# Attention and a mixture of experts on one core: the experts moved inside the branch, the second half ordered by hand, projections a slot later

## The chip, the cores and the metric

The kernel runs on one core of a Trainium2 chip (trn2). A core has a matrix engine (TensorE, PE), a vector engine (VectorE, DVE), a scalar engine with function tables (ScalarE, ACT), GpSimd (POOL), a queue engine that only issues transfers (SyncE, SP), an on-chip memory of 128 partitions (SBUF) and an accumulator memory of 8 banks (PSUM). The engines run on their own and wait for each other through semaphores. All data are float32. The metric is the time of one execution on the device, in microseconds (us).

## The reference

`x` is one sequence of 2048 rows of 512. The reference is an attention layer with residual and layer norm, and then a mixture of experts with residual and layer norm:

```python
q, k = unit_norm(q), unit_norm(k)           # 16 heads of 32; rotary positions on every second head
logits = einsum("bshd,bthd->bhst", q, k) * q_gain
y = causal_softmax(logits) @ v
x = layernorm(x + y @ w_out)
scores = softmax(x @ gate_w)                # 8 experts, the best 2 of each row
routed = sum over the 2 of  w_e * (silu(x @ w_gate[e]) * (x @ w_up[e])) @ w_down[e]      # 352 hidden
shared = (silu(x @ sw_gate) * (x @ sw_up)) @ sw_down                                     # 704 hidden
x = layernorm(x + routed + shared)
```

## The kernel before

**Attention.** `attention_then_moe` (L1384 on) loads `x` and the weights, works out whether the gains are small enough for a softmax with a fixed shift, and branches on it (`tc.If`, L1517). With the inputs here the first arm runs, `fast_attention`; the other, `general_attention`, is code that is jumped over. `sparse_moe` stands behind both arms.

`fast_attention` works in slots. Slot `n` is one unit of 160: a head group `g` of 4 heads, a block `b` of 512 queries, a tile `kt` of 128 keys. In a slot, PE makes the scores (L331), ACT the exponentials (L341), POOL the causal mask on the diagonal (L352), DVE and POOL the running sums (L370), and PE the product with the values (L379). Every engine runs in the order in which the code is written (`manual_schedule`, L477). Beside this, odd slots take one long step from `queue` (`long_step`, L443: a projection into q, k and v for a tile, L126, or, in the last head group, an output projection, L229), and even slots one short step from `shorts` (transposes, L204 and L271, and gates). `later(k, what)` puts a piece of work `k` slots on. A block's last value product starts `normalize` (L391): the sums over partitions (L397), their reciprocal, and `divide` (L417, L419). In the last head group `divide` puts the block's four output projections into `queue` at once (L426). In this phase, projections and transposes share one PSUM bank. When the last q, k, v projection is out of the queue, `x_is_read` (L450) loads the shared expert's weights into the place of the transposed `x`. After slot 160 a tail does what is left, filled up with six pieces of the shared expert's first block (`fillers`).

**Experts.** `sparse_moe` first finds each row's two experts and sorts the rows by expert (DVE, from L802). Meanwhile the shared expert's first half runs: eight tiles of 128 rows in blocks of two (`BT`); `shared_up(b, j)` makes piece `j` of 6 of the hidden rows (L667 on PE, L678 or L686 on ACT, L680 on DVE), and `shared_down(b)` the output (L975, and L981 for the last chunk, of half height). Then 36 tiles of routed rows are gathered, multiplied and written to `yd` in memory (`routed`, L1119). A second, inner branch (L1162) is for more tiles than usual, and isn't taken here.

The second half of the shared expert (L1169 on) takes blocks 4 to 7, and with them the rows of the first half whose shared part is kept in `accd`. For each of 16 tiles, `with_experts` (L1046) gathers the two expert rows with POOL's indirect transfers (L1049) and adds them on DVE (L1052); `finish` (L1054) normalizes on DVE (`layer_norm`, L779: two statistics, and a root by eleven small steps, L602 to L607) and stores (L1056). In slot 0 of each block SP reads the block's rows, the old rows and the next block's transposed rows (`read_block`, L948, 512 KB). Here only PE and SP run in the written order (`in_order`, L1079); for the other engines a planner chooses it. `yd` rows have 4 buffers (`m4`), the rows of `x` and of the sums 5 (`m5`).

Of the kernel before, what the change touches and what calls it, by code (L numbers as in the profile page):

```python
# [16 lines left out]
P = 128  # L17
S = 2048
DM = 512
# [22 lines left out]
def fast_attention(  # L42
    tc, mem, xT, xa, x, x1d, wq_sb, wo_sb, gain, rope_sb, gw, logits, ident, neg_gmax, small, x_is_read,
    x1T_kept, x1T_done, more_pieces,
):
# [13 lines left out]
    with (  # L59
# [331 lines left out]
        def normalize(g, b, y):  # L391
# [25 lines left out]
            def divide(rec, sign):  # L417
                by_tile = lambda a: a.rearrange("p (t m) -> p t m", t=TPB)
                nc.vector.scalar_tensor_tensor(  # L419
                    xa[:, b * TPB : (b + 1) * TPB, g * P : (g + 1) * P], by_tile(y), sign, by_tile(rec), ALU.mult, ALU.mult  # L420
                )
                if g == NC - 1:
                    if b == 0:
                        fetch(0)
                        fetch(1)
                    queue.extend((None, project(b * TPB + tl)) for tl in range(TPB))  # L426

# [15 lines left out]
        def long_step(n):  # L443
            if not queue or not may_start(queue[0][0], n):
                return False
            for step in queue.pop(0)[1]:
                step()
            if not read and (not queue or queue[0][0] is None):
                read.append(n)
                x_is_read()  # L450
            return True
# [25 lines left out]
        with tc.manual_schedule():  # L477
# [14 lines left out]
            banks(0, 2, 3)  # L492
            x_transposed(0)[0]()
            for i in range(EARLY * TPB):
                now[0] = i - EARLY * TPB
                tile_step(i)
                for what in due.pop(now[0], []):
                    what()
                for _ in range(2):
                    short_step(now[0])  # L500
# [6 lines left out]
            while n < NU or pending or queue or shorts or ends or due:  # L507
# [57 lines left out]
                n += 1  # L565
            assert not fillers

# [123 lines left out]

HID0 = 5 * GW

# [17 lines left out]
def sparse_moe(tc, big, shared, xs, ident, logits, w_gate, w_up, w_down, x1d, x1Td, x1T_kept, yd, accd, out):  # L711
# [12 lines left out]
    with (  # L724
# [10 lines left out]

        ones = mc.tile([P, P], F32, name="mones")
        nc.gpsimd.memset(ones, 1.0)

# [6 lines left out]

        hid_lent = [hidden(lent(CH * W)) for _ in range(2)]
        lent_early = lent(2 * P)
        last_down = big[:, DOWNS + (NE - 1) * DW :]
# [8 lines left out]
        nc.gpsimd.iota(table[:, 0, :], [[P, NTILES]], base=0, channel_multiplier=0)  # L757
        tile_starts = mc.tile([P, NTILES], F32, name="tile_starts")
        nc.vector.tensor_copy(tile_starts, table[:, 0, :])
# [18 lines left out]

        def layer_norm(dst, src, name):  # L779
            stats = m2.tile([P, 6], F32, tag="ln_stats", name=f"stats{name}")  # L780
            nc.vector.bn_stats(stats, src)  # L781
            mv = m2.tile([P, 2], F32, tag="ln_mv", name=f"mv{name}")
            nc.vector.bn_aggr(mv, stats)
            rstd = m2.tile([P, 1], F32, tag="ln_rstd", name=f"rstd{name}")
            inv_sqrt(nc, m2, rstd, mv[:, 1:2], EPS_LN, f"ln{name}")
            nc.vector.tensor_scalar(dst, src, mv[:, 0:1], rstd, ALU.subtract, ALU.mult)  # L786


# [14 lines left out]
        nc.scalar.activation(sc, sc, AF.Exp)  # L803
        rsum = mc.tile([P, NT], F32, name="rsum")
        nc.vector.reciprocal(rsum, reduced(sc, ALU.add, "lsum"))
# [146 lines left out]
        def hid_of(b):  # L952
            if b == 0:
                return hidden(big[:, HID0 : HID0 + CH * W])
            if b == NBL // 2 - 1:
                return hidden(spare[:, :])
            if b < NBL // 2:
                return hid_lent[b % 2]
            return hidden(big[:, (3 * BT * DM + b % 2 * CH * W) :][:, 0 : CH * W])
# [9 lines left out]

        def shared_down(b, done):  # L970
            hid = hid_of(b)
            pds = [ps_d.tile([P, DM], F32, tag="d", name=f"ps_ds{b * BT + tl}") for tl in range(BT)]
            for tl, pd in enumerate(pds):
                for j in range(CH - 1):
                    nc.tensor.matmul(  # L975
                        pd, hid[:, j, tl * P : (tl + 1) * P], wd[:, j, :], start=(j == 0), stop=False
                    )

            for tl, pd in enumerate(pds):
                rows = slice(tl * P // 2, (tl + 1) * P // 2)  # L980
                nc.tensor.matmul(  # L981
                    pd, hid[rows, CH - 1, tl * P : (tl + 1) * P], wd[rows, CH - 1, :], start=False, stop=True
                )
            for tl, pd in enumerate(pds):
                done(b * BT + tl, pd)

# [58 lines left out]

        def with_experts(t, acc):  # L1046
            for k in range(2):
                y = m4.tile([P, DM], F32, tag="y", name=f"y{k}_{t}")
                nc.gpsimd.indirect_dma_start(  # L1049
                    y, None, yd, bass.IndirectOffsetOnAxis(ap=slot_i[:, k, t : t + 1], axis=0)  # L1050
                )
                nc.vector.scalar_tensor_tensor(acc, y, tops[k][:, t : t + 1], acc, ALU.mult, ALU.add)  # L1052

        def finish(t, acc):  # L1054
            layer_norm(acc, acc, t)
            nc.sync.dma_start(out[0, t * P : (t + 1) * P, :], acc)  # L1056

        def read_rows(b):

            for t in range(b * BT, (b + 1) * BT):  # L1060
                row_of(t)
            for t in range(b * BT - HALF, (b + 1) * BT - HALF):
                held[t] = m5.tile([P, DM], F32, tag="row", name=f"old{t}")
                nc.sync.dma_start(held[t], accd[t * P : (t + 1) * P, :])
# [4 lines left out]
        def old_rows(t):  # L1069
            acc = held.pop(t)  # L1070
            with_experts(t, acc)
            finish(t, acc)

        def second_done(t, pd):
            acc = held.pop(t)
            nc.vector.tensor_tensor(acc, pd, acc, ALU.add)  # L1076
            finish(t, acc)

        in_order = lambda: tc.manual_schedule(engines={mybir.EngineType.PE, mybir.EngineType.SP})  # L1079
        with in_order():  # L1080
# [16 lines left out]
            for b in range(1, NBL // 2):  # L1097
                for j in range(CH):
                    shared_up(b, j)
                    if j == 0:  # L1100
# [67 lines left out]

        with in_order():  # L1169

            work = {}
            for b in range(NBL // 2, NBL):
                first = b * BT
                work[b] = [lambda t=first + k: early_rows(t) for k in range(BT)]
                work[b] += [lambda t=first - HALF + k: old_rows(t) for k in range(BT)]
            for b in range(NBL // 2, NBL):
                for j in range(CH):
                    if (b, j) != (NBL // 2, 0):
                        shared_up(b, j)
                    if j == 0:  # L1180
                        if b > NBL // 2:
                            shared_down(b - 1, second_done)
                        read_rows(b)
                        if b + 1 < NBL:
                            read_block(b + 1)
                    elif work[b]:
                        work[b].pop(0)()
            shared_down(NBL - 1, second_done)

# [195 lines left out]
def attention_then_moe(  # L1385
# [25 lines left out]

    big = const.tile([P, NE * EW], F32, name="big")
# [39 lines left out]

    def first_block(psum, acts):


        def piece(j):
            return lambda: shared_up_piece(
                nc, shared, x1T_kept[:, 0 : BT * DM], hidden(big[:, HID0 : HID0 + CH * W]), j,  # L1460
                lambda tag: psum(f"ps_{tag}s0_{j}")[:, 0:W], acts[j % 2],
            )

        return [piece(j) for j in range(CH)]

# [3 lines left out]

    with tc.tile_pool(name="aconst", bufs=1) as ac, tc.tile_pool(name="asmall", bufs=3) as asmall:  # L1470
        gain = ac.tile([P, NH], F32, name="gain")
# [19 lines left out]
        load_x(1)  # L1491
        rope_sb = ac.tile([P, NT, HD], F32, name="rope_sb")
        nc.sync.dma_start(rope_sb, rope.rearrange("(t p) r -> p t r", p=P))
# [23 lines left out]
        with tc.If(bounded > 0) as branch:  # L1517
            xT = shared[:, 0 : NT * DM].rearrange("p (t m) -> p t m", t=NT)
            fast_attention(
                tc, mem, xT, xa, x, x1d, wq_sb, wo_sb, gain, rope_sb, gw, logits, ident, neg_gmax, asmall, load_shared,  # L1520
                x1T_kept, x1T_done, first_block,
            )
        with branch.Else():
            general_attention(tc, mem, shared, x1d, xs, wq_sb, wo_sb, gain, rope_sb, ident, pow_mh, layer_norm, asmall)
            load_shared()
# [6 lines left out]
            with tc.tile_pool(name="ps_first", bufs=4, space=PSUM) as ps_first:  # L1532
                for piece in first_block(
                    lambda name: ps_first.tile([P, QB], F32, tag="f", name=name),
                    [mem[:, i * QB : i * QB + W] for i in (31, 32)],
                ):
                    piece()


    sparse_moe(tc, big, shared, xs, ident, logits, w_gate, w_up, w_down, x1d, x1Td, x1T_kept, yd, accd, out)  # L1540


# [41 lines left out]
```

## Time and profile before

| | |
|---|---|
| median of 3 runs | 1168.1 us (1167.95 to 1170.28) |
| the profiled execution | 1166.23 us, of which the span from first to last instruction 1164.5 |
| granted clock of PE, mean | 0.992 |
| attention, from the first matmul to the last logits | 5.8 to 636.8 us |
| shared expert's first half, sorting, weight loads | 640.5 to some 750 |
| 36 routed tiles | to 1035 |
| second half of the shared expert | 1036.5 to 1155.3 |
| after the last matmul, to the end of the span | 9.2 |

A row of the timeline has the start in the span, the duration, the engine, the line, the operation, what it writes and reads, how many such instructions are merged, and in brackets how long the engine stood idle before it and what ended that. A row of the waits has the waiting instruction, whom it waited for, the sum in us, the number and the longest. "issue" is time in which an engine waited for nothing that the profile shows. PEclk gives the granted clock of PE in tenths, in 40 slices of the span.

### The profile page before, as it was taken

The page shows a single profiled execution, that of the slowest core. Times are in us where ns is not written, and L with a number is a line of the kernel's source. Part 1 is how long each engine was busy: PE and PEld are TensorE (multiplying, and loading weights), DVE is VectorE, ACT ScalarE, POOL GpSimd, SP SyncE. Part 2 cuts the span into 40 slices and gives each one's busy share as a digit, 9 for nine tenths or more (in the row PEclk, how much of TensorE's full clock was granted, in tenths as well). Part 3 has the DMA queues.
Part 4 walks back from the last instruction along what each step waited for, and adds up shares of the span by engine and source line. Part 5 has one row for each costly group of instructions (what it writes and reads, how often), then busy time and mean ns, then how long its engine had stood idle before and what let it go on. Part 6 is the DMA issues. An engine that isn't in the chain of part 4 may idle for free. (4 is left out here: it accounts for less than half of the span.)

```text
span 1164.5 us, 15558 instructions
## 1 busy us (share of the span) xinstructions
PE 1115.0 (96%) x5692; PEld 584.5 (50%) x5692; DVE 617.5 (53%) x948; ACT 502.6 (43%) x847; POOL 366.6 (31%) x291
## 2 busy tenths in 40 slices
PE   7999999999999999988998999999999999999996
PEld 4533333333343333333355777556566565666664
DVE  1466797797888787787855341111111111115666
ACT  3677777878677777755651100112112121110000
POOL 0256684447645584322330010111010110012331
PEclk9999999999999999999999999999999999999999
DMA  9000000000000110212113496321122211033453
GB/s 305 12 1 1 1 1 1 1 1 1 2 1 2 46 54 2 73 55 73 55 47 120 166 329 204 115 64 64 64 73 64 64 64 55 36 118 99 155 163 126
DMA packets 50227, 83.71 MB, mean 72 GB/s; under 512 B 8032, under 2 KB 22368, under 8 KB 50144
## 3 DMA queue, kind: packets, MB, share of 16 engines
q1 hardware_dynamic: 43904, 64.39, 16.4%
q0 software_dynamic: 5440, 17.83, 5.3%
q8 instruction: 50, 0.82, 0.3%
q10 hardware_dynamic: 800, 0.39, 0.2%
q14 instruction: 33, 0.27, 0.1%
HBM read 59.79 MB, written 22.81 MB: 71 GB/s over the span
## 5 line engine op out<-in xcount | busy, mean ns | idle before, releaser
L341 ACT ACTIVATE big<-fps_s,neg_gmax 128x1024 f32<-128x1024 f32 (+3 forms) x320 | 297.1, 985 | 89.7 <-PE fps_s L331 88.3
L370 DVE TENSOR_TENSOR facc<-facc,big 128x1536 f32<-128x1536 f32 (+3 forms) x128 | 244.2, 1908 | 49.8 <-ACT big L341 25.1
L126 PE MATMUL fps_qkv<-big,shared 128*128 128x384 f32 x512 | 183.3, 502 | 1.9 <-ACT facc L406 0.8
L370 POOL TENSOR_TENSOR facc<-facc,big 128x512 f32<-128x512 f32 x72 | 142.3, 1976 | 104.1 <-ACT big L341 103.4
L331 PE MATMUL fps_s<-big 32*128 32x512 f32 (+3 forms) x1280 | 174.4, 580 | 0.7 <-ACT big L211 0.7
L379 PE MATMUL fps_av<-big 128*32 128x512 f32 (+3 forms) x1280 | 138.0, 537 | 15.6 <-POOL big L352 13.5
L126 PEld LDWEIGHTS fps_qkv<-big,shared 128*128 128x128 f32 x512 | 93.1, 192 | 85.6 <-issue 17.3
L1008 POOL DMA_INDIRECT rows<-x1d,rows_of x36 | 34.2, 949 | 260.1 <-PE ps_xT L1017 212.3
L1019 DVE COPY xT<-ps_xT 128x512 f32<-128x512 f32 x34 | 23.5, 692 | 171.4 <-PE ps_xT L1017 171.4
L331 PEld LDWEIGHTS fps_s<-big 32*128 32x128 f32 x1280 | 55.7, 183 | 92.6 <-issue 54.1
L1034 PE MATMUL ps_dr<-big,hT 128*128 (+1 forms) x216 | 98.8, 593 | 0.5 <-ACT hT L1027 0.5
L352 POOL TENSOR_SCALAR_AFFINE_SELECT big<-big 128x512 f32<-128x512 f32 x64 | 66.8, 1047 | 102.4 <-ACT big L341 97.4
L1042 ACT COPY y<-ps_dr 128x512 f32<-128x512 f32 x36 | 21.1, 586 | 166.3 <-PE ps_dr L1034 166.3
L1132 PE MATMUL ps_gr<-big,xT 128*128 x288 | 91.2, 459 | 0.0
L1132 PE MATMUL ps_ur<-big,xT 128*128 x288 | 91.2, 459 | 0.0
L379 PEld LDWEIGHTS fps_av<-big 128*32 128x32 f32 x1280 | 31.4, 109 | 109.1 <-issue 76.6
L678 ACT ACTIVATE acts<-ps_gs 128x256 f32<-128x256 f32 x35 | 13.4, 384 | 154.7 <-PE ps_gs L667 146.1
L667 PE MATMUL ps_us<-big,shared 128*128 128x256 f32 x336 | 78.6, 380 | 1.5 <-DVE big L680 1.5
L1049 POOL DMA_INDIRECT y<-yd,slot_i x32 | 36.3, 1135 | 133.2 <-DVE x L1052 62.5
L1132 PEld LDWEIGHTS ps_gr<-big,xT 128*128 128x128 f32 x288 | 54.5, 189 | 40.3 <-issue 17.1
L667 PE MATMUL ps_gs<-big,shared 128*128 128x256 f32 x280 | 68.6, 389 | 3.7 <-DVE big L763 3.7
L667 PEld LDWEIGHTS ps_us<-big,shared 128*128 128x128 f32 x336 | 63.6, 190 | 10.9 <-DVE big L680 2.3
(190 smaller groups left out, 1216.1 us busy)
## 6 DMA issues: line engine op xcount, KB each, us to landing
yd<-y SPq DMA_DIRECT2D x36, 256.0 KB
big<-in_L_ffn_w_gate_dram SPq DMA_DIRECT2D x8, 704.0 KB
big<-in_L_ffn_w_up_dram SPq DMA_DIRECT2D x8, 704.0 KB
big<-in_L_attn_x_dram SPq DMA_DIRECT2D x16, 256.0 KB
fres<-in_L_attn_x_dram SPq DMA_DIRECT2D x16, 256.0 KB
x1d<-big SPq DMA_DIRECT2D x16, 256.0 KB
big<-in_L_ffn_w_down_dram SPq DMA_DIRECT2D x8, 512.0 KB
x<-x1d SPq DMA_DIRECT2D x12, 256.0 KB
```

Source lines behind the costliest of these rows:

```text
L126: nc.tensor.matmul(ps[0], xT[:, t, c * P : (c + 1) * P], wq_sb[c].rearrange("p (s m) -> p s m", s=3)[:, :, g * P : (g + 1) * P], start=(c ...
L331: nc.tensor.matmul(pss[n][i // 2][:, i % 2, off:], k_at[(g * NB + kb) % KV][r, kl, :], q_at[u % Q][r, off:], start=True, stop=True,)
L341: nc.scalar.activation(pr_at[n % PR][:, 2 * j : 2 * j + 2, off:], pss[n][j][:, :, off:], AF.Exp, bias=neg_gmax)
L352: nc.gpsimd.affine_select(d, d, [[0, 4], [1, P]], ALU.is_ge, 0.0, base=0, channel_multiplier=-1)
L370: eng.tensor_tensor(acc[:, :, off:], first[:, :, off:], pr[:, hs, off:], ALU.add)
L379: nc.tensor.matmul(avs[g, b][32 * i : 32 * i + 32, off:], v_at[(g * NB + kb) % KV][:, kl, i * HD : (i + 1) * HD], pr_at[n % PR][:, i, off: ...
L667: nc.tensor.matmul(ps.rearrange("p (t m) -> p t m", t=BT), w[:, c, lo : lo + P], x[:, :, c, :], start=(c == 0), stop=(c == NC - 1),)
L1008: nc.gpsimd.indirect_dma_start(r, None, x1d, bass.IndirectOffsetOnAxis(ap=rows_of[:, i : i + 1], axis=0))
L1019: nc.any.tensor_copy(xT, pst)
L1034: nc.tensor.matmul(pd, hT[:w, c, :], big[:w, bass.ds(at_d + (DOWNS + c * DM), DM)], start=(c == 0), stop=(c == NHC - 1),)
L1049: nc.gpsimd.indirect_dma_start(y, None, yd, bass.IndirectOffsetOnAxis(ap=slot_i[:, k, t : t + 1], axis=0))
L1132: nc.tensor.matmul(ps, xT[:, c, :], big[:, bass.ds(at_e + (at + c * HE), HE)], start=(c == 0), stop=(c == NC - 1),)
```

## The change

1. At the start, 16 matmuls of the identity with itself run before the branch, and 6 more after the first transposes.
2. Output projections enter the queue one slot after `divide`; the load of the shared weights comes 8 slots after its trigger. The rotary table, which had SBUF of its own, lies in the shared weights' place, and other small tiles move too.
3. `sparse_moe` is called at the end of both arms of the branch. A seventh filler, the first piece of block 1, is made in the tail instead of in `sparse_moe`.
4. In the second half all five engines run in the written order. Slots 0 to 3 of a block issue gathers for the tile that is added two slots on; the tiles of the old rows come first. Statistics go to a table; the root is four steps on POOL with a power, and the scaling an ACTIVATE a slot later. Reads are spread: the block's rows in slot 2, the next block's transposed rows in slot 3, old rows in slot 5.
5. In the last block each of the two tiles is finished on its own, with the root's first guess by Ln and Exp on ACT.

```diff
-                    queue.extend((None, project(b * TPB + tl)) for tl in range(TPB))
+                    later(1, lambda: queue.extend((None, project(b * TPB + tl)) for tl in range(TPB)))
...
-                x_is_read()
+                later(8, x_is_read)
...
             x_transposed(0)[0]()
+            keep_busy(psum("fps_busy"), 6)
...
-            assert not fillers
+            while fillers:
+                fillers.pop(0)()
...
-        def shared_down(b, done):
+        def shared_down(b, done, apart=False):
...
+                if apart:
+                    rest(tl)
+                    done(b * BT + tl, pd)
...
+        def bring(t):
+            for k in range(2):
+                y = m4.tile([P, DM], F32, tag="y", name=f"y{k}_{t}")
+                nc.gpsimd.indirect_dma_start(
+                    y, None, yd, bass.IndirectOffsetOnAxis(ap=slot_i[:, k, t : t + 1], axis=0)
+                )
+                brought[t, k] = y
...
+        def statistics(t, acc):
+            stats = m2.tile([P, 6], F32, tag="ln_stats", name=f"stats{t}")
+            nc.vector.bn_stats(stats, acc)
+            nc.vector.bn_aggr(norm_at[:, 0:2, t], stats)
+
+        def roots(t, n):
+            nc.gpsimd.tensor_scalar(norms(2, t, n), norms(1, t, n), EPS_LN, None, ALU.add)
+            nc.gpsimd.tensor_tensor(norms(2, t, n), norms(2, t, n), norms(4, t, n), ALU.pow)
+            nc.gpsimd.tensor_tensor(norms(3, t, n), norms(0, t, n), norms(2, t, n), ALU.mult)
+            nc.gpsimd.tensor_scalar(norms(3, t, n), norms(3, t, n), -1.0, None, ALU.mult)
+
+        def scaled(t, acc):
+            nc.scalar.activation(acc, acc, AF.Identity, bias=norms(3, t), scale=norms(2, t))
             nc.sync.dma_start(out[0, t * P : (t + 1) * P, :], acc)
...
         def old_rows(t):
             acc = held.pop(t)
             with_experts(t, acc)
-            finish(t, acc)
+            statistics(t, acc)
+            roots(t, 1)
+            scalings.append((step[0] + 1, lambda: scaled(t, acc)))
...
+        def last_done(t, pd):
+            acc = held.pop(t)
+            nc.vector.tensor_tensor(acc, pd, acc, ALU.add)
+            statistics(t, acc)
+            seed = inv_sqrt_seed(nc, m2, norms(1, t), EPS_LN, f"ln{t}")
+            inv_sqrt_step(nc, m2, norms(2, t), norms(1, t), EPS_LN, seed, f"ln{t}")
+            nc.vector.tensor_scalar(acc, acc, norms(0, t), norms(2, t), ALU.subtract, ALU.mult)
+            nc.sync.dma_start(out[0, t * P : (t + 1) * P, :], acc)
...
-                    shared_up(b, j)
+                    if (b, j) != (1, 0):
+                        shared_up(b, j)
...
-        with in_order():
+        with tc.manual_schedule(engines={ET.PE, ET.SP, ET.DVE, ET.Pool, ET.Activation}):
...
                         if b > NBL // 2:
                             shared_down(b - 1, second_done)
+                        if b == NBL // 2:
+                            read_old(b)
+                    while scalings and scalings[0][0] <= step[0]:
+                        scalings.pop(0)[1]()
+
+                    if j == 2:
                         read_rows(b)
-                        if b + 1 < NBL:
-                            read_block(b + 1)
-                    elif work[b]:
-                        work[b].pop(0)()
-            shared_down(NBL - 1, second_done)
+                    elif j == 3 and b + 1 < NBL:
+                        read_block(b + 1)
+                    elif j == 5 and b + 1 < NBL:
+                        read_old(b + 1)
+                    if j >= 2:
+                        add, t = work[b][j - 2]
+                        add(t)
+                    if j < len(work[b]):
+                        bring(work[b][j][1])
+                    step[0] += 1
+            while scalings:
+                scalings.pop(0)[1]()
+
+            nc.scalar.activation(norms(2, 0), norms(4, 0), AF.Ln, scale=-1.0)
+            shared_down(NBL - 1, last_done, apart=True)
...
+    def keep_busy(ps, n):
+        for _ in range(n):
+            nc.tensor.matmul(ps[:, 0:P], ident, ident, start=True, stop=True)
...
+        keep_busy(ps_busy.tile([P, P], F32, name="busy"), 16)
...
+            moe()
         with branch.Else():
...
+            moe()
-    sparse_moe(tc, big, shared, xs, ident, logits, w_gate, w_up, w_down, x1d, x1Td, x1T_kept, yd, accd, out)
```

## The prediction

> **What bounds the kernel.** I read the page first, then the waits of PE over the whole span, then the timeline wherever a wait was longer than 2 us, and the chain of waits for the end.
>
> ```profile
> span 1164.5 us, 15558 instructions
> PE 1115.0 (96%) x5692; PEld 584.5 (50%) x5692; DVE 617.5 (53%) x948; ACT 502.6 (43%) x847; POOL 366.6 (31%) x291
> ...
> PEclk9999999999999999999999999999999999999999
> ```
>
> PE is busy for 1115.0 of 1164.5 us; every other engine is near half. So a stage's time is PE's work plus PE's gaps, and an edit is worth the gap it closes. The waits of PE (total, number, longest):
>
> ```profile
> PE fps_av L379 <- POOL big L352: 13.5, 15, 2.6
> PE fps_xT L112 <- POOL ones L68: 5.7, 1, 5.7
> PE ps_us L667 <- DVE big L680: 4.4, 3, 2.9
> PE ps_gs L667 <- DVE big L763: 3.7, 1, 3.7
> PE fps_x1T L271 <- DVE fres L239: 2.9, 1, 2.9
> PE fps_o L229 <- DVE big L419: 2.7, 1, 2.7
> ```
>
> The first row (causal masks on GpSimd) isn't touched; the other five are. A long gap costs twice, as the timeline shows at the start, at the join and in the second half:
>
> ```profile
> 7.57 5.09 PE L126 MATMUL fps_qkv<-big,shared 128*128 128x384 f32 x8 [0.74 <-ACT shared L113]
> ...
> 13.81 2.82 PE L126 MATMUL fps_qkv<-big,shared 128*128 128x384 f32 x8
> ...
> 640.03 0.23 DVE L763 CAST big<-big 128x128 f32<-128x128 int32 x1 [3.01 <-issue]
> 640.53 3.48 PE L667 MATMUL ps_gs<-big,shared 128*128 128x256 f32 x8 [3.74 <-DVE big L763]
> ...
> 1053.46 3.54 PE L667 MATMUL ps_us<-spare,shared 128*128 128x256 f32 x8 [2.89 <-DVE big L680]
> ```
>
> The same eight matmuls take 5.09 us cold and 2.82 warm; after gaps of 3.74 and 2.89 us a group takes 3.48 and 3.54 where the others take 1.89. So a gap of that length brings some 1.6 us of slow clock; gaps of 0.69 and 0.85 us further on bring none. At the end PE has finished and VectorE normalizes two tiles:
>
> ```profile
> 1155.24 0.69 DVE L1076 TENSOR_TENSOR x<-ps_ds,x 128x512 f32<-128x512 f32 x1 [0.57 <-PE ps_ds L981]
> ...
> 1160.62 0.98 SPq L1056 DMA_DIRECT2D out_dram<-x  x2
> 1160.70 0.55 DVE L786 TENSOR_SCALAR x<-x,mv,rstd 128x512 f32<-128x512 f32 x1
> ```
>
> **Start: 22 matmuls on the identity.** ident is ready at 1.54 us (its select: 1.26 + 0.28). The four cold transposes took 1.08 us, 0.27 each, so the first 16 fill 1.6 to 5.9, when the branch lets the transposes in (5.75 before). Six more, 1.6 us cold or 0.9 warm (0.15 each), lie beside ScalarE's copy, which left PE idle for 0.74. *Row:* before, PE started at 5.75 and was still slow at 12.2, after 6.4 us; from 1.6 that means warm at 8.0. The eight matmuls then start at 7.6 to 8.5 instead of 7.57 and take 2.8 instead of 5.09: gain 1.4 to 2.3. [...] The row is of this kernel but with a pause in it. I take 2.0 (1.0 to 2.8).
>
> **Projections a slot later.** In the last head group, each block's divide falls in an odd slot, where the queue is served next; with `later(1)` its first projection comes two slots on, so every projection takes the place of its successor. The ninth waited 2.71 us for L419 (548.0 to 550.70), and the groups behind it ran slow: 2.09 against 1.14, 2.31 against 1.92, 1.38 against 0.93, together 1.8. That projection's data will be ready: 4.5. The 2.93 us wait at 499.6 is a transpose caught behind a projection's add; the transpose moves away, but the next projection wants the same bank, free at 502.5. With scores first (1.14), 1.8 us of wait remain, probably without the slow clock (1.65): I count 1.0 of 2.7. Sum 5.5. The twelfth projection (3.70) moves from 574.3 to the slot at 581.5, whose diagonal units wait 2.8 us for masks anyway; as much leaves the slot at 477.5. Ends: 0, if VectorE, 81% busy from 500 to 580, is simply late elsewhere, and 7.5.
>
> The load of the shared weights now follows as one burst (3 x 1280 and 4 x 128 KB, 4.35 MB; 13 us at the 330 GB/s of the weight loads near 680) instead of trickling between 387 and 476. It enters SP's queue near 500, ahead of a residual row that VectorE adds near 517; the row lands about then. Their first reader is at 594.7. Hidden; 0 to 2 us if the row is late.
>
> **Experts inside the branches.** The jump over the other form goes from the middle to the end. Its price stands in the rows above: VectorE idle 3.01 us under "issue", ScalarE 2.29, PE 3.74 with 1.6 slow behind it. [...] By the row the join gives PE 5.3. The seventh filler (3.45 us of matmuls) then runs warm behind the last logits, and the first down product follows at 640.3 instead of 645.57; its hidden rows are ready at 636.1. (3.5 to 5.3: a PSUM bank still being read, or a second table load, may show.) At the end the jump lies beside the last output's landing: before, the last DMA was issued by 1161.6, and the span ended 2.9 us later with landing and barriers. After, jump 3.0 and then barriers, some 1.4: 4.4. I pay 1.5 (0 to 3).
>
> **Second half by hand.** PE lost here 2.89 + 0.85 + 0.69 and 1.65 slow, 6.1 us, each time since L680 stood on VectorE behind an add whose gathered row hadn't landed. Gathers are now issued two slots ahead (a slot is 3.45 us of PE), the eleven VectorE steps of a root go to four GpSimd steps, the scaling to ScalarE: those waits go; the 1.11 us of the inner branch at 1035.4 stays. What is late next is the read of the next block's transposed rows. It was issued in slot 0, some 25 us ahead; now SP reaches it in slot 3, behind the store of the first old tile, and that hangs on a chain from the end of the previous down product: adds and statistics of two tiles 3.2; roots 4 x 0.25; on GpSimd behind them two gathers, the second issued 1.25 later and landing after 4.4 (median of the gathers); two adds and statistics 1.6; roots 1.0; scaling and hand-over 0.75; store issue 0.4; block 3.5 (256 KB took 2.7 from issue, 256 KB more at 340 GB/s 0.75). Together 17.1 us against four slots and the last piece, 15.5: PE waits 1.6 us before blocks 6 and 7. Block 5, whose gathers start at 1038.65, is in time. So 3.2 lost instead of 6.1: gain 2.9. The unseen prices: no small arithmetic or power on GpSimd is in the trace. Below, an IOTA of 128x1, 0.13; above, the line through TENSOR_TENSOR of 256 and 512 columns (0.94, 1.26) cut at zero, 0.6; I take 0.25, nearer the tiny row. The chain holds eight of them. ScalarE's scaling: 0.7, from its 0.59 us copies of that size. Ends of this part: gain 6.1 (no wait) and loss 16 (third rival).
>
> **Last two tiles apart.** Before, PE's last matmul to VectorE's last step: 6.0 us for two tiles. After, the first tile's lies beside the second's matmuls. The second's: add 0.69, statistics 0.86, Ln 0.21, Exp 0.20, three steps 0.57, scaling 0.55, hand-overs 0.3, so 3.4; and one table load of 1.28 between Ln and Exp, since the dummy Ln names no set and the trace shows only loads for the function at hand; 0 if that set holds both. Against it, the half-height products no longer run side by side: 2 x 0.86 instead of 1.13, 0.6. Gain 6.0 - 4.7 - 0.6 = 0.7, 2.0 without the load.
>
> **Sum.** 2.0 + 5.5 + 5.3 + 2.9 + 0.7 - 1.5 = 14.9. The profiled execution took 1166.2 (1164.5 and 1.7 around it), which gives 1151.3; the median of the three runs stands 1.9 above it, at 1168.1, so the forecast is 1153.2.
>
> **Rivals.**
> *The waits only move.* VectorE, behind in the last head group, gives the projections' 5.5 back at the next bank, and the second half loses its old 6.1 in new places. For it: VectorE is 9 tenths busy in several of those slices. Against it: it idles 1.5 us right after the stall at 552. Left: 2.0 + 5.3 + 0.7 - 1.5 = 6.5, so 1161.6.
> *The block's read decides, and the kernel is slower.* GpSimd's small steps cost 0.6, gathers land after 5.3 (the slowest seen), the block after 5.0 in their traffic. The chain is then 22.3: PE waits 6.8 us before blocks 6 and 7 and 3.3 before block 5, each with 1.65 slow: 21.8 instead of 6.1. The other parts' 12.0 don't cover the 15.7: 1168.1 + 3.7 = 1171.8. It decides from 18 us of loss on, some 6 a block. For it: eight steps in a row on an engine whose price isn't seen. Against it: tiny GpSimd operations took 0.1.
> *It doesn't do what it says:* a jump may still stand between attention and experts, or PE may wait at the join for VectorE's softmax. Against it: count() comes twenty us later in PE's order. Then 5.3 go: 1158.5, inside the forecast's own range and its chance.
>
> **Numbers.** Forecast 0.55 (its own range 1147 to 1159); waits only move 0.24, both faster; the block's read 0.16; near no change 0.05. What a measurement can tell from no change is about 0.2%, 2.3 us. Faster 0.79, same 0.05, slower 0.16. The range 1146 to 1169 leaves out the third case and little else.
>
> **What will show it.** Start: L126's first eight matmuls near 2.8 us, not 5.1. Last head group: no wait of fps_o for L419. Join: no "issue" gap on VectorE, ps_ds following within 1 us of the filler. Second half: no wait for L680; waits of L667 for a DMA of x1Td, or none. GpSimd's rows give the price of a small step. End: one or two ACT_TABLE_LOADs between Ln and Exp, and 4 to 5 us from the last output's issue to the end. I am wrong if PE's gaps after 1036 add up to more than before, or if the attention part isn't shorter by at least 4 us.

## The result, and the profile after

The changed kernel takes 1180.4 us in the median of four runs (1178.15 to 1182.89), the kernel before, beside it, 1169.1 (1167.95 to 1170.28): a ratio of 1.0094, with a 95% interval of 1.0078 to 1.011. It is slower. The profiled execution took 1181.02 us, 1179.2 of it the span. The page, in its first lines and the clock:

```profile
span 1179.2 us, 15490 instructions
...
PE 1124.1 (95%) x5736; PEld 591.8 (50%) x5736; DVE 596.4 (51%) x764; ACT 518.8 (44%) x870; POOL 379.0 (32%) x336
...
PEclk9999999999999999999999999999999999998998
```

PE still bounds it. In the last four slices, the second half of the shared expert, the clock falls below nine tenths twice; before it didn't. The waits of PE name the place:

```profile
PE ps_gs L670 <- DMA big<-x1Td: 14.2, 3, 5.8
...
PE fps_x1T L271 <- DVE fres L239: 2.9, 1, 2.9
...
PE ps_ds L972 <- DVE big L690: 2.0, 1, 2.0
PE ps_us L670 <- DVE big L683: 1.6, 3, 0.6
```

The first row is new: before blocks 5, 6 and 7, PE stands still until the block's transposed rows have landed (2.9, 5.5 and 5.8 us). The old waits for L763, L419 and most of that for L680 (now L683) are gone; the one for L239 stayed. The account, from the starts of the same instructions in both traces (these two executions differ by 14.7 us, the medians by 11.3, because the profiled execution before, 1166.23, was quicker than its fellows):

| stretch | before | after | change | forecast |
|---|---|---|---|---|
| start to the first filler | 594.71 | 590.54 | -4.2 | -7.5 |
| filler to the second piece of block 4, so mainly the join | 441.78 | 437.48 | -4.3 | -5.3 |
| from there to PE's last matmul | 118.7 | 138.0 | +19.3 | -2.9 |
| PE's last matmul to DVE's last step | 6.0 | 7.7 | +1.7 | -0.7 |
| DVE's last step to the end | 3.25 | 5.4 | +2.2 | +1.5 |
| sum | | | +14.7 | -14.9 |

So 8.5 us are won by 1028 us, and the second half loses 21. The waits for x1Td, 14.2, and the slow matmuls behind them (3.57, 3.75 and 3.75 where the others take 1.89, so 5.4) make up 19.6 of these. Before, the read for block 7 went out 8.8 us after the down product of block 5, and PE started on it 6.8 us later with no wait:

```profile
1098.91 1.13 PE L981 MATMUL ps_ds<-shared,big 64*128 64x512 f32 x4
...
1108.83 0.42 SPq L950 DMA_DIRECT2D big<-x1Td  x1
...
1115.61 1.89 PE L667 MATMUL ps_gs<-big,shared 128*128 128x256 f32 x8
```

The same stretch, from the end of a down product to the start of the next block, in the timeline of the changed kernel, where the read goes out 17.6 us after it:

```profile
1098.91 0.69 DVE L1108 TENSOR_TENSOR x<-ps_ds,x 128x512 f32<-128x512 f32 x1 [7.62 <-PE ps_ds L972]
...
1102.15 0.24 POOL L1078 TENSOR_SCALAR big<-big 128x2 f32<-128x2 f32 x1 [17.22 <-DVE big L1074]
...
1102.48 0.73 POOL L1079 TENSOR_TENSOR big<-big 128x2 f32<-128x2 f32 x1
...
1105.38 0.95 POOL L1055 DMA_INDIRECT y<-yd,slot_i  x1 [0.30 <-issue]
...
1111.36 0.75 DVE L1063 SCALAR_TENSOR_TENSOR old<-y,top,old 128x512 f32<-128x512 f32 x1 [2.08 <-DMA y<-yd,slot_i]
...
1113.15 0.24 POOL L1078 TENSOR_SCALAR big<-big 128x1 f32<-128x1 f32 x1 [4.32 <-DVE big L1074]
...
1113.48 1.00 POOL L1079 TENSOR_TENSOR big<-big 128x1 f32<-128x1 f32 x1
...
1115.24 0.81 ACT L1084 ACTIVATE old<-old,big 128x512 f32<-128x512 f32 x1 [7.12 <-POOL big L1081]
...
1116.08 0.34 SPq L1085 DMA_DIRECT2D out_dram<-old  x1
...
1116.47 0.42 SPq L944 DMA_DIRECT2D big<-x1Td  x1
...
1121.21 3.75 PE L670 MATMUL ps_gs<-big,shared 128*128 128x256 f32 x8 [5.78 <-DMA big<-x1Td]
```

Read it as a chain: two tiles' adds and statistics on DVE until 1102; their roots on POOL; two gathers queued behind the roots, the second landing 5.98 us after its issue; the add that needed it; another root; ACT's scaling; SP's store; and only then, behind that store on SP, the read of the next block, and PE starts on it 4.74 us after that issue, 5.78 us after it has run out of work. The eight matmuls then take 3.75 instead of 1.89 us: the granted clock over them is 0.50. The tail:

```profile
1163.96 0.75 DVE L1063 SCALAR_TENSOR_TENSOR x<-y,top,x 128x512 f32<-128x512 f32 x1 [1.81 <-DMA y<-yd,slot_i]
...
1164.90 1.12 PE L972 MATMUL ps_ds<-shared,big 64*128 64x512 f32 x2
...
1166.64 1.28 ACT L618 ACT_TABLE_LOAD   x1
...
1171.10 1.28 ACT L618 ACT_TABLE_LOAD   x1
...
1173.21 0.55 DVE L1120 TENSOR_SCALAR x<-x,big 128x512 f32<-128x512 f32 x1
```

The last early tile's gather lands just before PE's last product, so the first of the two tiles, which was to be finished beside the second's matmuls, isn't; and both chains, now one behind the other, hold a table load before the Exp.

### The profile page after: what moved, and what is told of

It reads as the page before. It is cut to its first block, busy times and chain, and to the rows that moved or that the text cites. A ratio compares the mean times of both kernels' runs of the same rounds, so it can differ in the third digit from the quotient of the medians.

```text
span 1179.2 us, 15490 instructions
## 1 busy us (share of the span) xinstructions
PE 1124.1 (95%) x5736; PEld 591.8 (50%) x5736; DVE 596.4 (51%) x764; ACT 518.8 (44%) x870; POOL 379.0 (32%) x336
## 5 line engine op out<-in xcount | busy, mean ns | idle before, releaser
L379 PE MATMUL fps_av<-big 128*32 128x512 f32 (+3 forms) x1280 | 138.0, 537 | 14.5 <-POOL big L352 12.5
L126 PEld LDWEIGHTS fps_qkv<-big,shared 128*128 128x128 f32 x512 | 92.0, 190 | 83.5 <-issue 15.5
L352 POOL TENSOR_SCALAR_AFFINE_SELECT big<-big 128x512 f32<-128x512 f32 x64 | 63.4, 993 | 108.1 <-ACT big L341 103.0
L670 PE MATMUL ps_gs<-big,shared 128*128 128x256 f32 x280 | 72.4, 404 | 14.2 <-DMA big<-x1Td 14.2
L1177 PEld LDWEIGHTS ps_gr<-big,xT 128*128 128x128 f32 x288 | 54.5, 189 | 40.3 <-issue 17.1
L670 PEld LDWEIGHTS ps_gs<-big,shared 128*128 128x128 f32 x280 | 55.2, 202 | 28.0 <-ACT acts L689 15.3
```

The costliest lines, as they stand in the source:

```text
L126: nc.tensor.matmul(ps[0], xT[:, t, c * P : (c + 1) * P], wq_sb[c].rearrange("p (s m) -> p s m", s=3)[:, :, g * P : (g + 1) * P], start=(c ...
L352: nc.gpsimd.affine_select(d, d, [[0, 4], [1, P]], ALU.is_ge, 0.0, base=0, channel_multiplier=-1)
L379: nc.tensor.matmul(avs[g, b][32 * i : 32 * i + 32, off:], v_at[(g * NB + kb) % KV][:, kl, i * HD : (i + 1) * HD], pr_at[n % PR][:, i, off: ...
L670: nc.tensor.matmul(ps.rearrange("p (t m) -> p t m", t=BT), w[:, c, lo : lo + P], x[:, :, c, :], start=(c == 0), stop=(c == NC - 1),)
L1177: nc.tensor.matmul(ps, xT[:, c, :], big[:, bass.ds(at_e + (at + c * HE), HE)], start=(c == 0), stop=(c == NC - 1),)
```

## The experiments

Theory "order": what costs is the place of the block's read on SP, behind a store at the end of that chain. Rivals: its landing in the new traffic ("traffic"), GpSimd's slow steps as such ("roots"). Each ratio is to the kernel before, measured beside it.

**1. The read first.**

```diff
+                        if b + 1 < NBL:
+                            read_block(b + 1)          # in slot 0, ahead of everything
-                    elif j == 3 and b + 1 < NBL:
-                        read_block(b + 1)
```

> The changed kernel with one edit: the read of the next block's transposed rows goes from slot 3 to slot 0, ahead of all stores of that block. Theory 'order' (the read stands on SP behind the store of the first old tile, and that store hangs on gathers, adds and GpSimd's roots): PE's 14.2 us of waits for x1Td go to under 1 us, and with them the 5.4 us of slow clock behind them (3.57, 3.75 and 3.75 instead of 1.89 each); about 1161 us, 19 below 1180.4. Rival 'traffic' (the read lands late because of the gathers, row reads and stores beside it; moved, it delays these instead): PE waits elsewhere in the second half, for L690 or in the down products, and the time stays above 1172. Rival 'roots' (GpSimd's chain delays the whole block): waits fall by less than half.

Measured: 1162.5 us, ratio 0.9958 (0.9941 to 0.9975). The waits for x1Td are gone from PE's list; of the second half this is left:

```profile
PE ps_us L670 <- DVE big L683: 4.3, 3, 1.6
...
PE ps_ds L972 <- DVE big L690: 2.0, 1, 2.0
```

"Order" holds. The rows themselves landed no sooner after their issue (the three of this half in the median after 5.6 us, 4.5 in the changed kernel), and the roots are as they were: neither rival can explain it. A part of "traffic" may be true: the waits for L683 grew from 1.6 to 4.3. By the ratios this one edit brings back 16 us, so the kernel would then be 5 us quicker than the one before, still not the 14.9 of the forecast; the last part tells what the rest lost.

**2. Only the order on SP.**

```diff
+                    if j == 3 and b + 1 < NBL:
+                        read_block(b + 1)
                     while scalings and scalings[0][0] <= step[0]:
                         scalings.pop(0)[1]()
```

> The changed kernel with the read of the next block left in slot 3, but issued ahead of the store of that slot instead of behind it. Theory 'order', if the store alone holds SP: the read goes out at the time of slot 2's row reads, 6 us or more earlier, and the waits for x1Td go: 1161 to 1164 us. If SP already stands in slot 2 (stores of the previous block's tiles, row reads that wait for a buffer), a part remains, 1164 to 1172. Rival 'traffic': the landing takes longer and the waits stay, 1177 or more.

Measured: 1161.6 us, 0.9947 (0.993 to 0.9965), and no wait for x1Td. In the same slot, one place ahead of the store on SP's queue, the read is in time: for block 7 it goes out at 1097.21, not 1116.47, right behind the row reads,

```profile
1095.55 1.60 SPq L997 DMA_DIRECT2D x<-x1d  x2
...
1097.21 0.42 SPq L944 DMA_DIRECT2D big<-x1Td  x1
```

although it landed later after its issue than in the other two (median of the three 6.5). So the one store held SP, and nothing in slot 2.

**3. The suspected cost alone, in the kernel before.**

```diff
                         read_rows(b)
-                        if b + 1 < NBL:
-                            read_block(b + 1)
                     elif work[b]:
                         work[b].pop(0)()
+                        if j == 3 and b + 1 < NBL:
+                            read_block(b + 1)
```

> The kernel before with one edit: the read of the next block goes from slot 0 to slot 3, behind the store of the first old tile. It is the suspected cost alone, without GpSimd's roots and ScalarE's scaling. Theory 'order': that store waits there for a gather issued in the same slot (4.5), two adds (1.4) and the norm (3), so the read goes out 9.5 us into 10.3 us of slots and lands 4.5 later: PE waits about 4 us before blocks 5, 6 and 7, each with 1.7 of slow clock, 17 us more than before, about 1186. Rival 'roots' (the loss is that of GpSimd's steps): within 3 us of the kernel before, 1169 to 1172. Rival 'traffic': also little, since the old mix of transfers stays, 1169 to 1174.

Measured: 1205.3 us, 1.0329 (1.0303 to 1.0356). PE's longest list entry:

```profile
PE ps_gs L667 <- DMA big<-x1Td: 34.4, 3, 12.8
```

With no root on GpSimd at all the same wait appears, nearly three times as long as I expected (34.4 in all, against some 12): the store there hangs on a gather issued in its own slot, as expected; that the planner's order on DVE does the rest was not tried. So the place behind a store is enough; the changed kernel's own chain is shorter than the old one would be in that place.

**4. The table set for the end.**

```diff
-            nc.scalar.activation(norms(2, 0), norms(4, 0), AF.Ln, scale=-1.0)
+            nc.scalar.preload_act_table_set("natural_log_exp_and_others")
```

> The changed kernel with the dummy Ln at the end replaced by a preload of the table set that holds both Ln and Exp. Theory: no table load stands between Ln and Exp of the last two tiles, both loads of 1.28 us leave the chain of the last tile: 2.6 us less, 1177.8. Rival: the end hangs on the last tile's gathers and products, one of the two loads lies beside the other tile's work: 1.3 us or less, 1179 to 1180.4.

Measured: 1180.3 us, 1.0109 (1.0085 to 1.0133), against 1.0094 for the changed kernel: not told apart. In its profile all loads between Ln and Exp are gone, and PE's last matmul to DVE's last step takes 5.1 us instead of 7.7; a wait that is 1.0 longer in block 7 hides part of this.

**5. Without the identity matmuls.**

```diff
-            keep_busy(psum("fps_busy"), 6)
...
-        keep_busy(ps_busy.tile([P, P], F32, name="busy"), 16)
```

> The changed kernel without the 22 matmuls on the identity. Theory (they pay back little): the first transposes go back from 6.99 to about 5.75 us, the first eight matmuls of L126 from 2.75 to about 5.1, so the second transposes start about 1.0 later than 11.46; the slow clock between 60 and 100 us (0.96 in a slice, in the changed kernel alone) goes and gives 1.4 back, and the last matmuls of L126 start at about 471.3 instead of 471.7: between 0.5 faster and 1 slower, 1180 to 1181. The prediction's price, 2.0 us gained by them: 1182.4. Rival (the slow clock is another's): the 60 to 100 us slice stays at 0.96.

Measured: 1182.4 us, 1.0121 (1.009 to 1.0153), not told from 1.0094. In its profile the first eight matmuls take 4.55 us, and the second transposes start at 11.38, where with identity matmuls they start at 11.46. The clock between 60 and 100 us is 0.96 here too, so this run speaks against my theory of that slice; other profiles are less clear (last section).

**6. The expert layer once, behind both arms.**

```diff
-            moe()
         with branch.Else():
...
-            moe()
+    moe()
```

> The changed kernel with the expert layer built once behind both forms again, everything else as it is. Theory: the 3.7 us wait for L763 and the slow group behind it return (4.3 to 5.3 between the filler at 590.5 and the first down product), and the time from VectorE's last step to the end of the span falls from 5.4 to about 3.3: 2 to 3 us slower in sum, 1182.5 to 1183.5. Rival, the reading by which the jump is only moved: what the middle loses the end gives back, 1180 to 1181. If the end doesn't change, the longer end isn't the jump's and the time is 1184.7 or more.

Measured: 1183.7 us, 1.0124 (1.0092 to 1.0157), not told from 1.0094. The number lies close to what I expected, but the reason I gave isn't there. At the join the engines jump again, and PE doesn't care:

```profile
637.30 8.82 PE L978 MATMUL ps_ds<-shared,big 128*128 128x512 f32 x20 [0.76 <-DVE big L683]
637.60 1.28 ACT L797 ACT_TABLE_LOAD   x1 [2.36 <-issue]
...
640.40 0.23 DVE L766 CAST big<-big 128x128 f32<-128x128 int32 x1 [3.33 <-issue]
```

DVE's and ACT's gaps by "issue" are back, but PE is in the middle of a down product that needs neither. From the filler to the second piece of block 4 it takes 437.9 us instead of 437.5, and the end takes 3.2 instead of 5.4. What makes the profiled execution longer than that of the changed kernel is, above all, the waits for x1Td (16.1, not 14.2) and L690 and the slow clock behind them: after a wait of 2.8 us the last ten matmuls took 7.3 us instead of 4.6.

```profile
1165.16 1.72 PE L972 MATMUL ps_ds<-shared,big 64*128 64x512 f32 x2 [2.78 <-DVE big L690]
1166.81 7.31 PE L978 MATMUL ps_ds<-shared,big 128*128 128x512 f32 x10
```

**7. Projections queued at once, as before.**

```diff
-                    later(1, lambda: queue.extend((None, project(b * TPB + tl)) for tl in range(TPB)))
+                    queue.extend((None, project(b * TPB + tl)) for tl in range(TPB))
```

> The changed kernel with the projections queued as before (without the slot's delay). Theory: the ninth projection waits 2.7 us for L419 again with 1.6 to 1.8 of slow clock behind it, and the first filler starts 4.2 to 4.5 later than at 590.5: 1184.6. The eight projections ahead of it stay in their slots, the first one at 477.8. Rival 'the waits only move': the filler starts within 1 us of 590.5, and the time is 1180 to 1181.

Measured: 1185.8 us, 1.0141 (1.0108 to 1.0174; the interval just touches that of the changed kernel). The stall is back in the profile, with slow scores behind it, and the first filler starts at 596.58, 6.0 later:

```profile
551.09 2.07 PE L229 MATMUL fps_o<-big 128*128 128x512 f32 x2 [2.72 <-DVE big L419]
553.10 2.09 PE L331 MATMUL fps_s<-big 32*128 32x512 f32 x8
```

**8. A version without the chain:** the read in slot 0, the joint table set, and gathers three slots ahead of their adds and ahead of that slot's roots, into eight stretches of `big` that are free by then:

```diff
-                y = m4.tile([P, DM], F32, tag="y", name=f"y{k}_{t}")
+                at = DOWNS + len(order) % 8 * DM
+                order.append((t, k))
+                y = big[:, at : at + DM]
...
+                    while todo and todo[0][0] <= step[0] + 3:   # (slot of the add, tile)
+                        bring(todo.pop(0)[1])
                     if j >= 2:
                         add, t = work[b][j - 2]
                         add(t)
-                    if j < len(work[b]):
-                        bring(work[b][j][1])
```

> The changed kernel with three edits: the block's read in slot 0; gathers issued three slots ahead of their adds and ahead of that slot's roots, into eight free stretches of big instead of four buffers; the joint table set for the end. Theory 'order' for the gathers too (VectorE's adds wait for gathers that stand on GpSimd behind roots): the 4.3 us of waits for L683 and the 2.0 for L690 go, the last tiles' add follows its product at once, and VectorE's last step comes 3.5 to 4.5 us after PE's last matmul instead of 7.9: 1162.5 - 6.3 - 4.0 = 1152, 1150 to 1155. Rival 'traffic' (gathers under the reads of block and rows land later the earlier they all go out): waits for L683 stay above 3 us, 1157 or more.

Measured: 1151.0 us (1150.91 to 1151.96), 0.9854 (0.9828 to 0.988). From 1020 us on PE waits twice, 0.5 us just before the inner branch and 0.7 at it. The tail shows what the last step was meant to do:

```profile
1139.01 1.12 PE L972 MATMUL ps_ds<-shared,big 64*128 64x512 f32 x2
1140.17 0.69 DVE L1118 TENSOR_TENSOR x<-ps_ds,x 128x512 f32<-128x512 f32 x1 [2.27 <-PE ps_ds L972]
...
1142.89 0.55 DVE L1122 TENSOR_SCALAR x<-x,big 128x512 f32<-128x512 f32 x1
```

DVE is idle when PE's last product arrives, and 3.3 us later it is done, the 3.4 of the prediction without its table load.

**9 to 12. On this version, with no waits to blur it.** The expert layer once, behind both arms (the diff of experiment 6):

> The version with far gathers and the joint table set, with the expert layer built once behind both forms again. Without waits in the second half no slow clock blurs the comparison. Theory (the wait at the join went because the first piece of block 1 moved ahead of it, and nine us of down products that need nothing behind the join lie beside the other engines' jump): the middle is 0.2 slower, the end 2.2 shorter, 1151.0 - 2.0 = 1149.0. The prediction's price of the join (5.3 in the middle, 1.5 at the end): 1154.8. Rival 'the jump is only moved': 1151.

1150.7 us (1148.89 to 1152.5), 0.9856 (0.9835 to 0.9877): not told apart. Its profile loses 0.5 between the filler and the second piece of block 4, and gains 1.8 at the end (3.2 instead of 5.0). Next, experts in both arms, but the first piece of block 1 back in the expert layer:

```diff
-        return [piece(0, j) for j in range(CH)] + [piece(1, 0)]
+        return [piece(0, j) for j in range(CH)]
...
-                    if (b, j) != (1, 0):
-                        shared_up(b, j)
+                    shared_up(b, j)
```

> The version with far gathers and the joint table set, experts inside both branches, but the first piece of block 1 is no filler of the attention any more: it opens the expert layer again, as before the change. If the experts inside the branches are enough to take the wait away (the prediction's step): no wait of PE over 1 us between 634 and 650, 1150 to 1152. If the moved piece is what did it: PE waits 2 to 4 us again there, for VectorE or ScalarE's table load, 1153 to 1157.

1151.7 us (1150.66 to 1153.82), 0.9866 (0.9846 to 0.9886), and a wait of 0.28 us at the join. So either edit alone takes away the 3.7 us that PE waited there before. Last, without the identity matmuls (the diff of experiment 5), on both forms:

> The version with far gathers and the joint table set, without the 22 matmuls on the identity. The prediction's price (they gain 2.0): 1153.0. Theory (transposes start 1.2 to 2.5 earlier without them and the eight cold matmuls take 1.8 to 2.3 longer): within 0.8 of 1151, and the second transposes start between 11.3 and 12.5 in both.

> The version with far gathers, the joint table set and the expert layer built once, without the 22 matmuls on the identity: a third pair for the start, beside far_joined at 1150.7. If they gain what the prediction gave them, and what the medians of the first two pairs lean to (2.0 and 2.6): 1152.7 to 1153.3. If the profiles of those pairs are right, in which the first filler starts 0.9 earlier and 0.2 later without them: 1150 to 1151.

1153.5 us (1151.26 to 1156.11), 0.9883 (0.9865 to 0.99), and 1149.7 us (1149.56 to 1150.97), 0.9841 (0.9825 to 0.9857). Three pairs of medians give the 22 matmuls a gain of 2.0 and 2.6 and a loss of 1.1; the intervals of each pair overlap, so no gain is shown. The last of these kernels is the quickest measured, 1.6% below the kernel before.

## Why the prediction was wrong

**The failed step** is "Second half by hand", in its sum for the block's read: "17.1 us against four slots and the last piece, 15.5: PE waits 1.6 us before blocks 6 and 7". The chain was named link by link, and experiments 1 to 3 show that the place at its end, behind the store, is what costs. The mechanism was right; the terms were too small. Between blocks 6 and 7, in the rows above, a landing counted up to the start of the instruction that waited for it:

| term | forecast | measured |
|---|---|---|
| adds and statistics of two tiles | 3.2 | 3.2 |
| roots, twice | 2.0 | 1.66 + 2.05, and 0.3 of hand-over |
| two gathers: second issue, landing | 1.25 + 4.4 | 1.40 + 5.98 |
| adds and statistics before the second root | 1.6 | 1.7 |
| scaling, hand-over, store | 1.15 | 1.3 |
| the block's landing | 3.5 | 4.74 |
| sum | 17.1 | 22.3 |

The prediction also took it that the read had been issued some 25 us ahead before. That holds for none of the three: it was 18.2 us for block 5, and 6.8 for blocks 6 and 7 (1108.83 to 1115.61 above), so there was little room to move it back at all.

Against the 22.3 stood 16.5 us of work for PE, not 15.5, of which 0.55 is a wait for L683; hence 5.8 us and not 1.6. Block 5, which the forecast had in time, waited 2.9 us. Its chain is another: there the first add comes at 1035.82, in VectorE's written order behind a step of the shared expert (L683), and not behind a gather; roots, scaling, store and the read's 4.66 us follow.

```profile
1035.30 0.42 DVE L683 TENSOR_TENSOR big<-ps_us,acts 128x256 f32<-128x256 f32 x1 [3.03 <-PE ps_us L670]
1035.82 1.54 DVE L1063 SCALAR_TENSOR_TENSOR old<-y,top,old 128x512 f32<-128x512 f32 x2
...
1042.03 0.38 SPq L944 DMA_DIRECT2D big<-x1Td  x1
...
1046.69 3.57 PE L670 MATMUL ps_gs<-big,shared 128*128 128x256 f32 x8 [2.86 <-DMA big<-x1Td]
```

The rival "the block's read decides" had the mechanism and nearly the waits: 6.8, 6.8 and 3.3 against 5.8, 5.5 and 2.9. That its sum was 22.3 too is luck: its roots were too dear (4.8 against 3.7), its gather too quick (5.3 against 5.98). Its 1171.8 was still too low: in the account above the stretch up to PE's last matmul lost 19.3, not 15.7, and the other parts won 4.6, not the 12.0 that it left them.

Two rows were the wrong ones to price from. The median of the gathers seen before was 4.4; of all gathers after it is 4.9, but the one on the chain, which goes out beside two stores and two row reads, took 5.98 (5.89 a block earlier). And 0.25 for a small GpSimd step missed the power, which takes 0.57 to 1.00. Where a chain's slack is negative by estimate, each later link adds in full, and each wait of 2.9 us or more cost another 1.7 to 1.9 of slow clock; that I had counted for the rival, but not in the forecast. How much of the wait would go with the gathers or the roots alone moved was not tried.

**Start** (gain 2.0). Not shown. The matmul groups ran warm, 2.75 instead of 5.09, but the 22 matmuls took longer than I gave them: I priced each like a transpose, which leaves one record, and each leaves two. The first 16 leave 32 records of 5.67 us in all, and the transposes began at 7.10:

```profile
1.59 5.67 PE L1480 MATMUL busy<-ident 128*128 128x128 f32 x32 [1.59 <-POOL ident masks.py:199]
...
7.10 0.60 PE L112 MATMUL fps_xT<-ident,big 128*128 128x128 f32 x4
...
7.54 1.50 PE L1480 MATMUL fps_busy<-ident 128*128 128x128 f32 x12
...
8.88 2.75 PE L126 MATMUL fps_qkv<-big,shared 128*128 128x384 f32 x8
```

A warm record takes 0.125 (12 in 1.50), so 32 would take 4.0. If a cold one takes twice that, as the matmuls at a granted clock of 0.50 did at 1121.21 (3.75 against 1.89), 5.67 holds by estimate 3.3 us of cold clock; by the same estimate the nine profiles with these matmuls (5.25 to 6.76) span 2.5 to 5.5. All of this is read from durations: the granted clock of the profile is 1.00 over the whole start, before as after, so the cold clock itself is not shown there. The estimates lie below my row of 6.4, which had a pause in it. The sum's 2.0 stands inside the row's own gain of 1.4 to 2.3; the 2.8 at the upper end of my range is shown by no run: the runs showed eight matmuls 2.3 us shorter behind transposes 1.35 later. What I missed was the price of the matmuls, 1.35 us of delay for the first transposes, and 1.50 where PE had been idle for 0.74.

**Projections** (5.5). The ninth one's part came (it runs at 551.61 with no wait): together with the start it brings the first filler 4.2 earlier, where 4.5 were forecast for it alone. The 1.0 at 499.6 didn't: when block 0's `divide` came (467.23), the queue still held a projection into q, k and v (471.70), so its first output projections stayed in their slots (477.83; 477.46 before) and the wait for L239 is 2.9 as before. Taking the edit out costs 6.0 up to the first filler and 5.4 in the median. The burst of shared weights hid, as forecast.

**Join** (5.3). 4.3 came. But experiments 6, 9 and 10 show two causes, each enough, where the prediction priced one: experts inside the arms, or a first piece moved ahead, which leaves 9 us of down products beside the jump. That the right cause was named for these 4.3 is therefore half luck. With the experts inside the arms the jump comes at the end, beside the last store's landing, and the end is 1.8 to 2.2 us longer (5.0 and 5.4 against 3.2; forecast 1.5).

**Last two tiles** (0.7 gained). 1.7 lost: late gathers put the tiles one behind the other, and so there were two loads on the path, not one, since Ln and Exp each called their own set back. Without both, experiment 8 has it at 3.3 us instead of 6.0.

## What to carry to other kernels

When a read is moved later on an in-order queue, write down the store or wait ahead of it and follow that back to its start; if the estimated slack is small beside the spread of the links, take the slowest landing seen, not the median, and add the slow clock. Here the repair was one line: issue first what PE waits for. An edit that hides a jump and one that moves it can buy the same microseconds, so price them together, and against the end.

## What the runs showed of the hardware

- A 128x128 f32 matmul of the identity leaves two records (32 for 16, 12 for 6), a transpose of the same size one (4 for a tile's four). Record for record they take the same when warm: 12 of either in 1.50 and 1.47 us.
- GpSimd's steps on one or two columns in the changed kernel: 0.24 for an add or a product with a constant (once 0.75), 0.19 to 0.51 for a product, 0.57 to 1.00 for a power. The power on two columns (0.73) took no longer than on one.
- The 512 KB reads of transposed rows (x1Td) landed 4.2 to 4.6 us after issue in the changed kernel, and up to 7.1 in experiment 2. Gathers of 256 KB from `yd` landed after 3.6 to 6.7 in the changed kernel.
- A wait at the same place can bring unequal slow clock: behind 2.0 us before the last product, the ten matmuls took 4.56 in the changed kernel; behind 2.8 in experiment 6, 7.31. There the wait is also longer. But at the 2.65 us gap near 88 us, which is in the profiles of the kernel before, the changed kernel and experiments 5, 8 and 11, the clock of the slice from 60 to 100 us stayed at 1.00 in four of the five profiles without the identity matmuls, and fell to 0.96 or below in the nine with them. In the changed kernel:

```profile
87.48 1.08 PE L379 MATMUL fps_av<-big 128*32 128x256 f32 x8 [2.65 <-POOL big L352]
88.49 2.09 PE L331 MATMUL fps_s<-big 32*128 32x512 f32 x8
```

Before, these two groups took 0.64 and 1.14 behind the same gap. It is a sign that what 22 matmuls win at the start is in part given back there; why was not tried.
